# Cross-attention on one core: scaling the attended values instead of the exponentials

## The chip, the cores and the metric

The kernel runs on one core of a Trainium2 chip. The metric is device time in microseconds for one execution. The core has five engines that matter here: TensorE (PE in the profile, its weight loads PEld), VectorE (DVE), ScalarE (ACT), GpSimd (POOL) and SyncE (SP), which issues nearly all DMAs in the order of its own queue.

## The reference

A layer of cross-attention over 8 sequences of 256 rows, with 256 keys each, width 1024, 32 heads of 32, all in 32-bit floats:

```python
x = (hidden_states - mu) * rsqrt(var + LN_EPS) * ln_gamma + ln_beta
Q = split_heads(x @ Wq.T); K = split_heads(memory_keys); V = split_heads(memory_values)
scores = einsum('bhsd,bhtd->bhst', Q, K) * HEAD_DIM ** (-0.5)     # masked with -inf
probs = softmax(scores, axis=-1)
attn = einsum('bhst,bhtd->bhsd', probs, V)                        # heads joined again
out = hidden_states + attn @ Wout.T
```

Keys and values are the same tensor (the context).

## The kernel before, in words

**Quads.** Four heads of 32 fill the 128 partitions, so the unit of work is a quad of four heads of one sequence: 8 quads a sequence, 64 in all, numbered n = 8b + i. The main loop runs over n. Nothing is reordered by a scheduler: the order of each engine's queue is the order in which the program is written, and semaphores are set from the data that instructions share.

**One iteration n**, on TensorE: the scores of quad n + 1 (`scores`, L486, into four PSUM tiles `sc`), the attended values of quad n - 2 (`values`, L636, into two PSUM tiles `pv`), then parts of the query projection for a later sequence (L345 and L447) and of the output projection of the sequence before (`product_steps`, L720). From the second sequence on, both projections use a seven-product scheme on half-size blocks (names A11, S2, T4 and so on), whose sums of blocks POOL computes (`sum_x`, `sum_at`, `sum_wo`). The last sequence's output is made by `end_steps` (L787), partly in the last iterations (`po_last`) and partly after the loop (`po_end`, `po_end_s`).

**Softmax of quad n + 1** (`softmax_parts`), in the same iteration. For each head j and each half s of the rows, VectorE adds the mask and takes the row's extreme (L524), and ScalarE computes the exponentials `e` in place with their row sum `den` (`exps`, L528). `normalize(j)` takes the reciprocal of the sums (L535) and multiplies `e` by it, per partition: on POOL mostly (L543), on VectorE for j = 1 of quads 8 to 15, on ScalarE for j = 3 of quads 1 to 15 (L538). `blocks(j)` transposes the exponentials in blocks of 32 x 32 on VectorE into `pT` (L549). `aside` lets ScalarE copy half of `pT` to `pc` (L555), and `tail` issues the DMAs that exchange halves between partitions (`pT<-pT` L614, `pT<-pc` L618), with the loads of later keys, values and rows between them. In quads 0 to 7 and 57 to 63 the tail is put off into the next quad's softmax.

**Attended values.** `copy_at` lets ScalarE copy `pv` to `at` (L649), one iteration after the quad's softmax is complete. A tile `at` holds four quads (half a sequence), and it is the operand of the output projection.

**After the loop** TensorE works through products of the last sequence in written order: `values(61)`, `po_end` of quads 60 and 61, `values(62)`, `po_last`, `po_end_s` (from sums made by `end_sum` on POOL, L779), `values(63)`, and the rest. VectorE adds products to the rows (`end_add`, L793), and SP stores them (L1070).

## Time and profile before

| what | value |
|---|---|
| runs | 567.67, 567.94, 568.49 us (median 567.94) |
| profiled execution, first to last instruction | 566.0 us, granted clock of TensorE 1.000 |
| instructions | 20200 |
| chain that ended last | 97% TensorE |
| POOL multiplying exponentials by `rden` (L543) | 466 x 479 ns = 215.4 us |
| VectorE reciprocals (L535) | 256 x 150 ns = 38.2 us |
| ScalarE copies `at<-pv` (L649) | 128 x 253 ns = 26.1 us |

The profile page and the trace describe one execution, whose own time is the span in the table; the time of a run, measured around the execution, is 1.9 us more at the median. A row of groups reads: line, engine, operation, output <- input, shapes, count | busy us in all, mean ns of one | idle time before them and what ended it. A row of the timeline or of the chain begins with its start in us from the span's start and its duration; for a DMA on SP's queue (SPq) the duration is that of the issue, and the time to landing stands in the DMA views.

### The profile page before, as it was taken

What the parts mean: (1) busy time and instruction counts of PE and PEld (TensorE: products, weight loads), DVE (VectorE), ACT (ScalarE), POOL (GpSimd) and SP (SyncE); (2) the same over time, 40 slices, a digit from 0 to 9 for tenths busy, and PEclk for the clock granted to TensorE, in tenths of its full rate; (3) what the DMA queues carried; (4) which work ended last, traced back from release to release, by engine and by line L of the source; (5) the groups of instructions that cost most, each with busy time, mean ns of one, the idle gap of its engine ahead of it and who ended that gap; (6) DMA issues with size and microseconds to landing.
All of it is one profiled execution on the core that took longest, in us unless ns stands there. A gap on an engine that the chain in (4) does not pass through costs nothing.

```text
span 566.0 us, 20200 instructions
## 1 busy us (share of the span) xinstructions
PE 561.4 (99%) x7266; PEld 393.7 (70%) x7266; DVE 467.6 (83%) x1716; ACT 423.4 (75%) x1464; POOL 394.3 (70%) x636
## 2 busy tenths in 40 slices
PE   8999999999999999999999999999999999999997
PEld 8788886767766767667766776667766767755454
DVE  5889889999988988878898888988888777879923
ACT  4699999997778866786777876778776776769820
POOL 2788887899777656857568665777648657448780
PEclk9999999999999999999999999999999999999999
DMA  8966667856697777966778767796658864536751
GB/s 310 397 181 199 185 198 228 281 162 179 212 301 232 223 202 235 263 195 191 233 216 239 215 176 221 230 273 193 176 140 269 255 191 128 146 110 180 218 156 74
DMA packets 47219, 119.02 MB, mean 210 GB/s; under 512 B 8976, under 2 KB 9744, under 8 KB 47120
## 3 DMA queue, kind: packets, MB, share of 16 engines
q1 hardware_dynamic: 46976, 117.74, 69.5%
q8 instruction: 57, 0.93, 0.8%
q14 instruction: 42, 0.34, 0.2%
q10 hardware_dynamic: 144, 0.01, 0.0%
HBM read 66.33 MB, written 11.53 MB: 138 GB/s over the span
## 4 chain that ended last, share of the span: by engine, by line
PE 97%; DMA 1%; DVE 0%; POOL 0%; ACT 0%; issue 0%; SPq 0%; POOLq 0%
PE po_S L720 21%; PE pq_A L447 19%; PE pv L636 12%; PE sc L486 12%; PE po_A L720 11%; PE pq L345 9%; PE pq_S L447 8%; PE po_end L787 3%; PE po_last L787 1%; DMA x<-in_x_dram 1%; PE po_end_s L787 0%; POOL x L885 0%; PE pq L290 0%; PE px L307 0%; ACT e L528 0%; PE px L273 0%
## 5 line engine op out<-in xcount | busy, mean ns | idle before, releaser
L543 POOL TENSOR_SCALAR e<-e,rden 128x256 f32<-128x256 f32 x466 | 215.4, 479 | 125.5 <-DVE rden L535 123.0
L528 ACT ACTIVATE e<-e,mn 128x256 f32<-128x256 f32 x512 | 254.0, 502 | 46.1 <-DVE mn L524 44.9
L549 DVE STREAM_TRANSPOSE pT<-e 128x512 f32<-128x512 f32 x256 | 178.9, 703 | 35.6 <-POOL e L543 27.5
L524 DVE CUSTOM_DVE_ANT_0 e<-sc,mb 128x256 f32<-128x256 f32 x512 | 185.3, 415 | 25.4 <-PE sc L486 25.1
L555 ACT COPY pc<-pT 128x512 f32<-128x512 f32 x128 | 79.0, 617 | 55.7 <-DVE pT L549 35.6
L528 ACT ACTIVATION_READ_ACCUMULATOR e<-e,mn 128x1 f32 x512 | 98.4, 192 | 0.0
L486 PEld LDWEIGHTS sc<-k,qa 32*128 32x128 f32 x1024 | 46.1, 184 | 42.2 <-issue 21.6
L720 PE MATMUL po_S<-wo,at 128*128 128x512 f32 x152 | 74.3, 606 | 0.0
L636 PE MATMUL pv<-pT,v 64*32 64x128 f32 x4096 | 74.1, 274 | 0.0
L486 PE MATMUL sc<-k,qa 32*128 32x256 f32 x1024 | 73.6, 401 | 0.1
L636 PEld LDWEIGHTS pv<-pT,v 64*32 64x32 f32 x4096 | 57.0, 105 | 22.5 <-issue 11.8
L720 PE MATMUL po_A<-wo,at 128*128 128x512 f32 x128 | 59.4, 605 | 0.0
L345 PE MATMUL pq<-xnT,wq 128*128 128x256 f32 (+1 forms) x240 | 55.0, 384 | 0.0
L447 PEld LDWEIGHTS pq_A<-xnT,wq 128*128 128x128 f32 x416 | 48.5, 192 | 6.2 <-issue 4.8
L345 PEld LDWEIGHTS pq<-xnT,wq 128*128 128x128 f32 x240 | 44.6, 190 | 8.2 <-issue 1.5
L720 PE MATMUL po_S<-wo,s 128*128 128x512 f32 x104 | 50.1, 606 | 0.0
L447 PE MATMUL pq_A<-xnT,wq 128*128 128x128 f32 x416 | 48.5, 275 | 0.0
L535 DVE RECIPROCAL rden<-den 128x2 f32<-128x2 f32 x256 | 38.2, 150 | 7.3 <-ACT e L528 6.2
L524 DVE DVE_READ_ACCUMULATOR2_ANT mn<- 128x1 f32 x512 | 42.4, 83 | 0.0
L720 PEld LDWEIGHTS po_A<-wo,at 128*128 128x128 f32 x128 | 22.9, 189 | 25.6 <-issue 24.5
L720 PEld LDWEIGHTS po_S<-wo,at 128*128 128x128 f32 x152 | 25.5, 190 | 19.5 <-issue 19.5
L753 POOL TENSOR_TENSOR r<-r,p 128x512 f32<-128x512 f32 x24 | 30.6, 1277 | 4.8 <-ACT e L528 3.0
(102 smaller groups left out, 666.1 us busy)
## 6 DMA issues: line engine op xcount, KB each, us to landing
v<-in_kv_dram SPq DMA_DIRECT2D x32, 512.0 KB, 4.2
pT<-pT SPq DMA_DIRECT2D x128, 128.0 KB, 2.9
pT<-pc SPq DMA_DIRECT2D x128, 128.0 KB, 4.0
ring<-kept_T SPq DMA_DIRECT2D x20, 512.0 KB, 5.3
k<-in_kv_dram SPq DMA_DIRECT2D x32, 256.0 KB, 4.1
x<-in_x_dram SPq DMA_DIRECT2D x15, 512.0 KB, 5.6
r<-in_x_dram SPq DMA_DIRECT2D x28, 256.0 KB, 4.5
out_dram<-r SPq DMA_DIRECT2D x28, 256.0 KB, 3.2
```

What stands on the lines that cost most here:

```text
L345: nc.tensor.matmul(pqs[n], wq[:, o, c, :], xnTs[b](c), start=(c == 0), stop=(c == NC - 1),)
L447: nc.tensor.matmul(pqs[b][:, o, :], w[:, c], x_[:, c], start=begins and o + c == 0, stop=c == NK - 1, skip_group_check=True,)
L486: nc.tensor.matmul(scs[n][j][:, s, :], qa[r, n % NQ, ts(s, P)], ks[n - n % 2][r, n % 2, :], start=True, stop=True,)
L524: nc.vector.tensor_tensor_reduce(out=e[:, s, :], in0=pss[j][:, s, :], in1=mbs[n // NQ], scale=1.0, scalar=NO_SCORE, op0=ALU.add, op1=ALU.m ...
L528: nc.scalar.activation(e[:, s, :], e[:, s, :], AF.Exp, bias=mn[:, s : s + 1], scale=-1.0, accum_out=den[:, s : s + 1],)
L535: nc.vector.reciprocal(rden, dens[j])
L543: engine.tensor_scalar(es[j][:, s, :], es[j][:, s, :], rden[:, s : s + 1], 1.0, ALU.mult, ALU.mult,)
L549: nc.vector.transpose(pT[:, :, :, j, :, :].rearrange("p a i s k -> p (a i) s k"), es[j].rearrange("p s (b t) -> p b s t", t=K),)
L555: nc.scalar.copy(pc[:, :, ts(j, 2)], pT[:, 1, :, ts(j, 2)])
L636: nc.tensor.matmul(pvs[n][r][j * HD : (j + 1) * HD], vs[n - n % 2][ts(r, 2 * K), i, ds(n % 2 * P + j * HD, HD)], pT[ts(r, 2 * K), :, i, j, ...
L720: nc.tensor.matmul(po, operand(b, name)[:, c], wo[:, which, c], start=begins and c == 0, stop=c == NK - 1, skip_group_check=not begins,)
L753: nc.gpsimd.tensor_tensor(r, r, p1s[b], ALU.add)
```

## The change

Exponentials stay unscaled. The sums of four quads (128 rows x 4 heads x 4 quads x 2 halves) are collected in one tile `den`; when the fourth quad's sums are there, `send_dens` takes one reciprocal of 128 x 32, transposes it in blocks, writes it to a DRAM tile `sent`, and reads it back four times, once for each head, with each row given to the 32 partitions of that head, into `rB`. The attended values of a quad are multiplied by `rB` after they have been copied: in place on POOL (`scale_at`, quads 0 to 61), or on VectorE in place of ScalarE's copy (`copy_at_scaled`, quads 62 and 63). The products of `po_last` with quad 56 move from iteration 59 to iteration 60. `pc` has two buffers for three, and `rB` has one.

```diff
-    asp = ctx.enter_context(tc.tile_pool(name="asp", bufs=3))
+    asp = ctx.enter_context(tc.tile_pool(name="asp", bufs=2))
+    rbp = ctx.enter_context(tc.tile_pool(name="rbp", bufs=1))
...
+    dens, rBs = {}, {}
+    sent = dram.tile([P, K], F32, tag="sent", name="sent_dens")
...
+        h, quad = divmod(n, NK)
+        if quad == 0:
+            dens[h] = sm.tile([P, NH, NK, NS], F32, tag="den", name=f"den_{h}", bufs=2)
+        den = dens[h]
...
-                    accum_out=den[:, s : s + 1],
+                    accum_out=den[:, j, quad, s : s + 1],
...
-        def normalize(j):
-            rden = sm.tile([P, NS], F32, tag="rden", name=f"rden_{n}_{j}")
-            nc.vector.reciprocal(rden, dens[j])
...
+        def send_dens():
+            rden = sm.tile([P, K], F32, tag="rden", name=f"rden_{h}", bufs=1)
+            rdenT = sm.tile([P, K], F32, tag="rdenT", name=f"rdenT_{h}", bufs=1)
+            nc.vector.reciprocal(rden, den.rearrange("p j c s -> p (j c s)"))
+            nc.vector.transpose(rdenT, rden)
+            nc.sync.dma_start(sent, rdenT)
+            rBs[h] = rbp.tile([P, NA, NK, NS, K], F32, tag="rB", name=f"rB_{h}")
+            of = sent.rearrange("(a j i) k -> j a i k", a=NA, j=NH)
+            for j in range(NH):
+                nc.sync.dma_start(
+                    rBs[h][ts(j, HD)].rearrange("p a c s k -> p a (c s) k"),
+                    of[j : j + 1].to_broadcast([HD, NA, NK * NS, K]),
+                )
...
         blocks(2)
+        if quad == NK - 1:
+            send_dens()
...
+    def scale_at(n, engine):
+        h, c = divmod(n, NK)
+        at = ats[divmod(h, 2)][:, c]
+        engine.tensor_tensor(at, at, rBs[h][:, :, c].rearrange("p a s k -> p s a k"), ALU.mult)
+
+    def copy_at_scaled(n):
+        h, c = divmod(n, NK)
+        for r, pv in enumerate(pvs.pop(n)):
+            a = ts(r, 2)
+            nc.vector.tensor_tensor(
+                ats[divmod(h, 2)][:, c, :, a, :], pv.rearrange("p a s k -> p s a k"),
+                rBs[h][:, a, c].rearrange("p a s k -> p s a k"), ALU.mult,
             )
...
+        if n >= 2 and (n - 2) % NK:
+            for one in range(n - 3 if (n - 2) % NK == 1 else n - 2, n - 1):
+                scale_at(one, nc.gpsimd)
...
-            end_steps(last, "A11", B11, (c,), (0,))
+            for one in {0: (), 1: (0, 1)}.get(c, (c,)):
+                end_steps(last, "A11", B11, (one,), (0,))
...
     values(N - 2)
-    copy_at(N - 2)
+    copy_at_scaled(N - 2)
...
     values(N - 1)
-    copy_at(N - 1)
+    copy_at_scaled(N - 1)
```

All calls of `normalize` go with it. The order of the last four quads in time: quad 63's softmax lies in iteration 62, so `send_dens` of quads 60 to 63 is issued there; `scale_at(60)` and `scale_at(61)` stand in iteration 63, ahead of the remaining adds and sums on POOL; and TensorE's list after `values(61)` is as before.

More of the change, by code (lines that the diff above doesn't have):

```diff
@@ L495, in xattn_kernel @@
     tails = []
-    BY_ACT = range(1, 2 * NQ)
-    BY_DVE = range(NQ, 2 * NQ)
     def softmax_parts(n, copies=(), ahead=(), between=(), hooks={}, fill=()):
@@ L514, in softmax_parts @@
         pc = asp.tile([P, NI, NH, NS, K], F32, tag="pc", name=f"pc_{n}")
-        es, mns, dens = {}, {}, {}
+        es, mns = {}, {}
+        h, quad = divmod(n, NK)
+        if quad == 0:
+            dens[h] = sm.tile([P, NH, NK, NS], F32, tag="den", name=f"den_{h}", bufs=2)
+        den = dens[h]
         def exps(j, part=range(NS)):
@@ L520, in exps @@
                 mns[j] = sm.tile([P, NS], F32, tag="mn", name=f"mn_{n}_{j}")
-                dens[j] = sm.tile([P, NS], F32, tag="den", name=f"den_{n}_{j}")
-            e, mn, den = es[j], mns[j], dens[j]
+            e, mn = es[j], mns[j]
             for s in part:
@@ L529, in exps @@
                     e[:, s, :], e[:, s, :], AF.Exp, bias=mn[:, s : s + 1], scale=-1.0,
-                    accum_out=den[:, s : s + 1],
+                    accum_out=den[:, j, quad, s : s + 1],
                 )
-        def normalize(j):
-            rden = sm.tile([P, NS], F32, tag="rden", name=f"rden_{n}_{j}")
-            nc.vector.reciprocal(rden, dens[j])
-            for s in range(NS):
-                if j == NH - 1 and n in BY_ACT:
-                    nc.scalar.activation(
-                        es[j][:, s, :], es[j][:, s, :], AF.Copy, scale=rden[:, s : s + 1]
-                    )
-                    continue
-                engine = nc.vector if j == 1 and n in BY_DVE else nc.gpsimd
-                engine.tensor_scalar(
-                    es[j][:, s, :], es[j][:, s, :], rden[:, s : s + 1], 1.0,
-                    ALU.mult, ALU.mult,
+        def send_dens():
[10 more added lines that the diff above has]
+                    of[j : j + 1].to_broadcast([HD, NA, NK * NS, K]),
                 )
@@ L565, in softmax_parts @@
                 exps(j, (1,))
-            normalize(0)
             fill_in()
@@ L577, in softmax_parts @@
             exps(2)
-            normalize(0)
             exps(3)
@@ L591, in softmax_parts @@
             hook()
-        if n not in BY_DVE:
-            normalize(2)
         fill_in()
-        if n in BY_ACT:
-            normalize(3)
         blocks(1)
         aside(0)
-        if n not in BY_ACT:
-            normalize(3)
         fill_in()
         blocks(2)
+        if quad == NK - 1:
+            send_dens()
         while fill:
```

3 lines of the change are left out of this document (removed).

## The prediction

> **What bounds the kernel now.** I read the page first (span, busy shares, the chain), then the waits of TensorE, then the chain in order of time, and last the timeline of the end, engine by engine.
>
> ```profile
> span 566.0 us, 20200 instructions
> PE 561.4 (99%) x7266; PEld 393.7 (70%) x7266; DVE 467.6 (83%) x1716; ACT 423.4 (75%) x1464; POOL 394.3 (70%) x636
> PE 97%; DMA 1%; DVE 0%; POOL 0%; ACT 0%; issue 0%; SPq 0%; POOLq 0%
> ...
> PE busy L119 <- POOL ring masks.py:199: 1.3, 1, 1.3
> PE px L273 <- DVE ring L884: 0.2, 1, 0.2
> ...
> 286.89 1.91 PE po_S L720 x4
> 354.82 1.91 PE po_S L720 x4
> 422.75 1.92 PE po_S L720 x4
> ```
>
> TensorE is busy for 561.4 of 566.0 us, the chain that ends last is 97% TensorE, and its only two waits (1.3 and 0.2 us) lie in the first 7 us. A busy matmul can hide a stall, so I looked at the chain in order of time: the same product begins at 286.89, 354.82 and 422.75, twice 67.93 us apart. A stream that waited for other engines would not keep a period to the hundredth. I conclude that TensorE runs one fixed list of matmuls without a gap, and that the time is the length of that list plus some 3 us at the end. The change leaves that list as it is but for one step that comes one iteration later. So nothing that it takes from other engines can come back as time, and the question is only where it makes TensorE wait.
>
> **What is removed.** Times are those of the profiled execution.
>
> ```profile
> L543 POOL TENSOR_SCALAR e<-e,rden 128x256 f32<-128x256 f32 x466 | 215.4, 479 | 125.5 <-DVE rden L535 123.0
> L535 DVE RECIPROCAL rden<-den 128x2 f32<-128x2 f32 x256 | 38.2, 150 | 7.3 <-ACT e L528 6.2
> L538 ACT ACTIVATE e<-e,rden 128x256 f32<-128x256 f32 x30 | 13.6, 504 | 2.3 <-DVE rden L535 2.2
> ```
>
> All 512 scalings of exponentials go: 466 on POOL (215.4 us), 30 on ScalarE (13.6 us), 16 on VectorE; so do 256 small reciprocals (38.2 us). Each transpose of exponentials then waits for ScalarE alone. None of this is on the path: value in time, zero. TensorE covers it all.
>
> **What is added in the body.** For each of 16 groups of four quads: one reciprocal and one small transpose on VectorE, five DMAs on SP's queue (`sent`, then four broadcasts `rB` that wait until it has landed), and multiplications of attended values: 62 on POOL, and for the last two quads four on VectorE in place of ScalarE's copies.
>
> ```profile
> L779 POOL TENSOR_TENSOR ring<-at,at x1: 734/734/734, 543.7 to 543.7; 128x256 f32<-128x256 f32 x1
> ...
> 242.04 1.15 SPq L614 DMA_DIRECT2D pT<-pT  x2
> 246.47 2.00 SPq L618 DMA_DIRECT2D pT<-pc  x2
> 260.21 1.16 PE L636 MATMUL pv<-pT,v 64*32 64x128 f32 x64
> ...
> 514.70 1.14 SPq L614 DMA_DIRECT2D pT<-pT  x2
> 517.06 1.15 SPq L618 DMA_DIRECT2D pT<-pc  x2
> 525.49 1.16 PE L636 MATMUL pv<-pT,v 64*32 64x128 f32 x64
> 532.14 1.16 PE L636 MATMUL pv<-pT,v 64*32 64x128 f32 x64
> ...
> L549 DVE STREAM_TRANSPOSE pT<-e 128x512 f32<-128x512 f32 x256 | 178.9, 703 | 35.6 <-POOL e L543 27.5
> L555 ACT COPY pc<-pT 128x512 f32<-128x512 f32 x128 | 79.0, 617 | 55.7 <-DVE pT L549 35.6
> ```
>
> A POOL product of 128x256 takes 0.73 us, so 62 take 45 us against 215 removed: POOL becomes lighter. It stands still, though, once in each group, until `rB` has landed, with its sums queued behind. In the body those sums are due one to three iterations (67.93 / 8 = 8.5 us each) later and no longer stand behind six to eight scalings, so they come no later than now: zero.
>
> SP is the queue that is really moved past. While it waits for `sent`, the ring loads and the copies between partitions (`pT`, L614 and L618) of the same quad wait behind it. By the prices worked out below this holds SP some 2.0 + 4 x 0.57 = 4.3 us from the time the sums are ready; the copies would anyway have waited for the last transpose and ScalarE's copy of it (0.7 + 0.6 us), so they start 3 us late. Quad 27 stands for the twelve groups in mid-kernel: L618 ends its issue at 248.5, lands about 4 us later at 252.5 (the median of these copies, quoted below), and TensorE first needs it at 260.21. Three us late, and up to 2 us more behind the broadcasts' own 512 KB, gives 257.5: hidden with 2.7 us to spare. Quad 59 is tighter, because the iterations at the end take only 6.65 us (525.49 to 532.14): issue ends at 518.2, landing 522.3, needed at 525.49. SP is free of `sent` and `rB` at about 515.8 there, 1.1 us after L614's place now, so the landing moves to 523.4, or 525.4 with the extra traffic: hidden, by 0.1 to 2 us. The third copy buffer of `pc` that goes is then reused one quad earlier, 17 us after its last use began; only ScalarE would wait, off the path. If this cover were gone, each late quad would cost what it is late; that is a rival below.
>
> **What is added at the end.** Here the values of the last four quads cannot be scaled before quad 63's sums exist, and TensorE wants the first of them almost at once.
>
> ```profile
> 537.05 0.50 ACT L528 ACTIVATE e<-e,mn 128x256 f32<-128x256 f32 x1
> 537.45 0.19 ACT L528 ACTIVATION_READ_ACCUMULATOR e<-e,mn 128x1 f32 x1
> 537.72 1.16 PE L636 MATMUL pv<-pT,v 64*32 64x128 f32 x64
> 538.80 3.70 PE L787 MATMUL po_end<-wo,at 128*128 128x512 f32 x8
> ...
> 534.38 1.14 SPq L614 DMA_DIRECT2D pT<-pT  x2
> 536.63 1.95 SPq L618 DMA_DIRECT2D pT<-pc  x2
> ...
> out_dram<-x_again SPq DMA_DIRECT2D x1, 64.0 KB, 1.6
> ...
> pT<-pT SPq DMA_DIRECT2D x128, 128.0 KB, 2.9
> pT<-pc SPq DMA_DIRECT2D x128, 128.0 KB, 4.0
> v<-in_kv_dram SPq DMA_DIRECT2D x32, 512.0 KB, 4.2
> ...
> L1070 SPq DMA_DIRECT2D out_dram<-x_again x5: 332/332/332, 557.8 to 563.5; - x5
> ...
> DMA to landing us min/median/max: 2.2/2.3/4.9
> ```
>
> The last row is that of the `pT` copies between 505 and 545 us.
>
> At 538.80 TensorE begins the output products of quad 60 (`po_end`, L787). Now it must first see quad 60 multiplied by `rB`. The steps, each with its row:
>
> 1. Quad 63's last sum is read out at 537.45 + 0.19 = 537.64. These exponentials are paced by the scores before them, which TensorE delivers at the same time as now, so this stays.
> 2. Reciprocal and small transpose on VectorE: no row has a 128x32 transpose; between the small reciprocal's 0.15 and the 128x512 transpose's 0.7 us. Either way about 538.0 to 538.5, and SP is busy with quad 62's copies until 536.63 + 1.95 = 538.58. `sent` is issued at 538.6.
> 3. `sent`, 16 KB in rows of 128 B to DRAM. Nearest: the 64 KB output store, 1.6 us, alone on the DMAs; above it 2.9. Here the tail of L618 is still moving, so 2.0 us: 540.6.
> 4. Three more issues on SP at 1.14 / 2 = 0.57 us before the fourth broadcast goes: 542.3. The lower end is 0.33 us an issue, as SP's last output stores take.
> 5. Landing of 128 KB: 2.9 us is the median of the same size between partitions; 4.2, that of 512 KB, is what all four together could need, 2.2 the least seen at the end. I take 2.9: 545.2.
> 6. One POOL product, 0.73 us: 545.9.
>
> So TensorE stands from 538.80 to 545.9: 7.1 us. Ends: 538.6 + 1.6 + 1.0 + 2.2 + 0.73 = 544.1, a stall of 5.3; 538.6 + 2.9 + 1.7 + 4.2 + 0.73 = 548.1, a stall of 9.3. Below 5.3 the rows exclude it: two transfers in series and a product come after 537.64.
>
> [...]
>
> What follows is not late again.
>
> ```profile
> 540.05 2.50 POOL L746 TENSOR_TENSOR r<-r,ends 128x512 f32<-128x512 f32 x2
> 543.52 3.70 PE L787 MATMUL po_last<-wo,at 128*128 128x512 f32 x8
> 547.06 1.88 PE L787 MATMUL po_end_s<-wo,ring 128*128 128x512 f32 x4
> ```
>
> Quad 61's product is done 0.73 us after quad 60's, while quad 60's two products last half of the 3.7 us that the row of 538.80 shows for both quads. POOL's end sums now stand behind this wait: 545.9 + 0.7 (quad 61) + 2.5 (two residual adds) + 0.73 = 549.8, and TensorE asks for the first (`po_end_s`, now at 547.06) 8.3 us after `po_end` begins, so at 554.2. Quad 62 is multiplied on VectorE under the 3.7 us of `po_last`. So the whole tail moves by 7.1 us and nothing else grows.
>
> **The sum.** 0 in the body + 7.1 at the end. The profiled span becomes 573.1; the shown runs have their median 1.9 us above this span (567.94), which I keep: 575.0 us.
>
> **Rivals.**
>
> *A: the broadcasts clog the queue.* 128 partitions read the same 16 KB; if that takes some 3 us longer than step 5, the tail stalls by 10.1 and quad 59's copies are 1 to 3 us late for TensorE: about 567.94 + 10.1 + 2 = 580. From 3 us on, the mid-kernel quads stall too, by the excess over the 2.7 us spare, twelve times. For: no row shows a broadcast. Against: step 5's rows, where transfers of that size or four times it land in 2.2 to 4.9 us amid other traffic. Chance 0.11.
>
> *B: faster, because busy is not bound.* The row of TensorE's weight loads says 70%, and waits with other engines' names stand before them.
>
> ```profile
> PEld sc L486 <- DVE pT L549: 8.3, 11, 0.8
> PEld pv L636 <- ACT pc L555: 6.3, 19, 0.3
> PEld sc L486 <- DVE rden L535: 3.4, 5, 0.8
> PEld pv L636 <- ACT e L528: 2.7, 7, 0.8
> ```
>
> If these 20.7 us were true waits for the softmax, earlier transposes would return them, and 567.94 + 7.1 - 20.7 = 554.3. It decides from the point where more than 7.1 us of them is real. [...] This trace speaks against it: the unbroken period, and one quad's values taking 1.16 us at 260.21, 525.49 and 537.72, whatever went on beside them. The weight loads run beside matmuls and wait for their turn. Chance 0.04.
>
> *C: no change.* The broadcast is hidden, within 1.1 us. `rB` would have to land by 539.2, 1.5 us after the last sum; one transfer alone takes longer. Chance 0.03.
>
> **How the numbers follow.** Forecast 0.82, A 0.11, B 0.04, C 0.03. The forecast's own range is 567.94 + 5.3 to + 9.3, 573.2 to 577.2; I take it up to 578.5 for the mild half of A. Faster by over 0.2% (1.1 us, about what a measurement of this kernel can tell from no change) is B, 0.04; within it C, 0.03; slower 0.93.
>
> **What would show it.** In the changed profile: the period of 67.93 us unchanged; one TensorE wait of about 7 us before the first `po_end` product, released by POOL's multiplication of `at`; that one waiting for a DMA into `rB`; `sent` issued near 538.6; POOL busy some 170 us less. Wrong would be: TensorE idle before `pv` in the body (A), a shorter period (B), or no gap before `po_end` (C).

## The result, and the profile after

The changed kernel takes 610.8 us (median of 4 runs, 610.3 to 611.4) against 568.1 us for the kernel before (4 runs beside it, 567.7 to 568.5): a ratio of 1.075, 95% interval 1.0735 to 1.0766. The forecast was 575.0, range 573.2 to 578.5. The direction was right; the loss is 42.7 us, not 7.1.

The page of the changed kernel, its span, busy shares and the chain's shares:

```profile
span 608.5 us, 19634 instructions
PE 574.3 (94%) x7266; PEld 399.8 (66%) x7266; DVE 440.3 (72%) x1480; ACT 406.7 (67%) x1430; POOL 223.8 (37%) x232
PE 68%; DMA 16%; DVE 6%; ACT 3%; SPq 3%; issue 3%; POOL 2%; DVEq 0%; POOLq 0%; ACTq 0%
```

TensorE has the same 7266 matmuls, but the chain is 68% TensorE where it was 97%, and 16% of it is DMA. POOL is 170 us lighter, as forecast, and the kernel is slower. The chain in order of time shows at once that the loss isn't only at the end:

```profile
332.55 1.91 PE po_S L726 x4
405.07 1.91 PE po_S L726 x4
477.62 1.91 PE po_S L726 x4
```

The period of a sequence, 67.93 us before, is 72.5 us here. TensorE's waits, the two large rows of before being 1.3 and 0.2 us (columns: waiter, releaser, us in all, times, longest):

```profile
PE pv L628 <- DMA pT<-pc: 10.1, 7, 3.2
PE po_end L793 <- POOL at L648: 8.8, 1, 8.8
PE po_S L726 <- DVE r L768: 6.3, 7, 1.3
PE pq_S L448 <- DMA ring<-kept_T: 2.6, 2, 1.6
```

The wait of 8.8 us before `po_end` was forecast. The others were not: values that wait for the copies between partitions, output products that wait for the residual rows, query products that wait for ring loads. All three hang on DMAs of SP's queue that have nothing to do with the broadcast's data.

To split the loss I compare when TensorE begins the values of quad 61: at 537.72 before (the row is in the prediction), at 568.71 after.

```profile
568.71 1.16 PE L628 MATMUL pv<-pT,v 64*32 64x128 f32 x64
568.99 0.35 DVE L538 RECIPROCAL rden<-den 128x32 f32<-128x32 f32 x1 [0.27 <-ACT e L530]
569.37 0.21 DVE L539 STREAM_TRANSPOSE rdenT<-rden 128x32 f32<-128x32 f32 x1
569.61 0.33 SPq L540 DMA_DIRECT2D sent_dens<-rdenT  x1
573.08 1.76 SPq L544 DMA_DIRECT2D rB<-sent_dens  x4
577.86 1.41 POOL L648 TENSOR_TENSOR at<-at,rB 128x256 f32<-128x256 f32 x2 [12.33 <-DMA rB<-sent_dens]
578.63 6.37 PE L793 MATMUL po_end<-wo,at 128*128 128x512 f32 x8 [8.77 <-POOL at L648]
584.93 1.16 PE L628 MATMUL pv<-pT,v 64*32 64x128 f32 x64
```

568.71 - 537.72 = 31.0 us are lost in the body. The values of quad 62 began at 542.44 before and begin at 584.93 here, 42.5 us later, so the end costs 11.5 us more: the stand of 8.77, and 2.7 because the eight `po_end` products, 3.70 us before, take 6.37. After that nothing more is lost.

Below, "body" is always the start of the values of quad 61 less 537.72; "middle" is that part of it which arises between quads 9 and 57, where the groups of mid-kernel lie; and "end" is the further shift of the values of quad 62. Each is the difference of starts in two traces.

**Where the body loses it.** The timelines of the changed kernel on SP, TensorE and POOL behind the group that ends with quad 23:

```profile
223.08 0.33 SPq L540 DMA_DIRECT2D sent_dens<-rdenT  x1
225.22 1.74 SPq L544 DMA_DIRECT2D rB<-sent_dens  x4
...
232.35 3.76 SPq L333 DMA_DIRECT2D xnT<-xe  x6
...
241.80 2.33 SPq L606 DMA_DIRECT2D pT<-pT  x2
...
245.28 0.43 SPq L150 DMA_DIRECT2D r<-in_x_dram  x1
```

```profile
245.25 1.87 PE L628 MATMUL pv<-pT,v 64*32 64x128 f32 x64 [1.88 <-DMA pT<-pc]
...
253.67 0.70 PE L726 MATMUL po_S<-wo,s 128*128 128x512 f32 x1 [0.71 <-DVE r L768]
```

```profile
251.62 1.27 POOL L759 TENSOR_TENSOR r<-r,p 128x512 f32<-128x512 f32 x1 [6.25 <-DMA r<-in_x_dram]
```

The group itself holds SP 4 us (223.08 to 226.96), near the 4.3 forecast, and no product waits there. The bill comes two iterations later: six `xnT` copies, then the copies of the next quads, then the load of residual rows, all in SP's order. At 245.25 TensorE stands 1.88 us for a quad's copies; the residual load goes out at 245.28, POOL waits 6.25 us for it, VectorE for POOL, and TensorE for VectorE. In mid-kernel nearly all steps of the body lie at quads 8b + 7 to 8b + 9, around and after the group of quad 8b + 7. After the other group of a sequence TensorE loses nothing there.

SP's own stands, over the same four middle sequences, before (217.8 to 489.5 us) and after (226.2 to 519.9 us):

```profile
SPq L618 <- DMA pT<-pT: 37.7, 27, 4.5
SPq L614 <- ACT pc L555: 31.7, 19, 3.2
SPq L412 <- PE pq_A L447: 11.6, 7, 2.3
SPq L614 <- ACT e L528: 10.7, 8, 3.6
SPq L412 <- PE pq_S L447: 2.4, 2, 1.3
```

```profile
SPq L610 <- DMA pT<-pT: 62.5, 27, 6.0
SPq L544 <- DMA sent_dens<-rdenT: 14.0, 8, 2.7
SPq L606 <- ACT e L530: 9.4, 18, 1.1
SPq L606 <- ACT pc L556: 0.9, 2, 0.5
```

A stand for ScalarE (rows L614 before, L606 after) means that SP was early: it had nothing left to do but to wait for data. That slack was 31.7 + 10.7 = 42.4 us in four sequences, and 10.3 are left. The stands of ring loads for TensorE (rows L412) are slack of the same kind, since SP waits there for a buffer that is still in use: 11.6 + 2.4 = 14.0 us before, 1.1 after. Together 56.4 us of slack became 11.4. SP now stands 14.0 us for `sent` and 62.5 - 37.7 = 24.8 us more for landings of `pT`; its issues, added up over the four sequences, grew from 160 to 186 us. That is 65 us more in a queue that had 56 us to spare. 45 us of it were paid out of the slack; the other 20 are near the 293.7 - 271.7 = 22 us by which the four sequences became longer.

The windows of the same four sequences (columns: stretch, length, busy time of the five engines, granted clock, DMA share, GB/s), before, then after:

```profile
217.80:489.50 271.70, 271.70 (x3684) 192.17 (x3680) 226.69 (x837) 203.44 (x714) 182.35 (x316) 1.00 0.72 209
```

```profile
226.20:519.90 293.70, 278.85 (x3691) 195.54 (x3690) 211.66 (x722) 200.99 (x714) 88.60 (x94) 0.99 0.75 214
```

The 16 DMA engines were busy for 72% of the time before, a share that the prediction left out. 0.75 x 293.7 - 0.72 x 271.7 = some 25 us of their time were added.

### The profile page after: what moved, and what is told of

Read it like the earlier page. It is cut to its first block, busy times and chain, and to the rows that moved or that the text cites. A ratio compares the mean times of both kernels' runs of the same rounds, so it can differ in the third digit from the quotient of the medians.

```text
span 608.5 us, 19634 instructions
## 1 busy us (share of the span) xinstructions
PE 574.3 (94%) x7266; PEld 399.8 (66%) x7266; DVE 440.3 (72%) x1480; ACT 406.7 (67%) x1430; POOL 223.8 (37%) x232
## 4 chain that ended last, share of the span: by engine, by line
PE 68%; DMA 16%; DVE 6%; ACT 3%; SPq 3%; issue 3%; POOL 2%; DVEq 0%; POOLq 0%; ACTq 0%
PE po_S L726 18%; PE pq_A L448 16%; PE sc L489 8%; PE pv L628 8%; DMA r<-in_x_dram 6%; PE pq L346 5%; DMA ring<-kept_T 4%; PE pq_S L448 4%; PE po_end L793 3%; PE po_A L726 3%; ACT e L530 2%; DVE pT L550 2%; DMA pT<-pT 1%; DVE e L526 1%; SPq L606 1%
## 5 line engine op out<-in xcount | busy, mean ns | idle before, releaser
L526 DVE CUSTOM_DVE_ANT_0 e<-sc,mb 128x256 f32<-128x256 f32 x512 | 181.8, 418 | 56.2 <-PE sc L489 56.0
L550 DVE STREAM_TRANSPOSE pT<-e 128x512 f32<-128x512 f32 x256 | 167.8, 689 | 9.9 <-ACT e L530 9.8
L648 POOL TENSOR_TENSOR at<-at,rB 128x256 f32<-128x256 f32 x62 | 44.6, 731 | 241.8 <-DMA rB<-sent_dens 126.1
L628 PE MATMUL pv<-pT,v 64*32 64x128 f32 x4096 | 77.5, 274 | 11.1 <-DMA pT<-pc 10.1
L628 PEld LDWEIGHTS pv<-pT,v 64*32 64x32 f32 x4096 | 58.6, 105 | 35.8 <-issue 27.0
L726 PE MATMUL po_A<-wo,at 128*128 128x512 f32 x128 | 61.3, 621 | 0.0
L346 PE MATMUL pq<-xnT,wq 128*128 128x256 f32 (+1 forms) x240 | 54.9, 383 | 1.1 <-ACT qa L355 1.1
L526 DVE DVE_READ_ACCUMULATOR2_ANT mn<- 128x1 f32 x512 | 42.5, 83 | 0.0
L726 PEld LDWEIGHTS po_S<-wo,s 128*128 128x128 f32 x104 | 17.7, 189 | 21.7 <-issue 15.0
```

The source lines that it names most:

```text
L346: nc.tensor.matmul(pqs[n], wq[:, o, c, :], xnTs[b](c), start=(c == 0), stop=(c == NC - 1),)
L526: nc.vector.tensor_tensor_reduce(out=e[:, s, :], in0=pss[j][:, s, :], in1=mbs[n // NQ], scale=1.0, scalar=NO_SCORE, op0=ALU.add, op1=ALU.m ...
L550: nc.vector.transpose(pT[:, :, :, j, :, :].rearrange("p a i s k -> p (a i) s k"), es[j].rearrange("p s (b t) -> p b s t", t=K),)
L628: nc.tensor.matmul(pvs[n][r][j * HD : (j + 1) * HD], vs[n - n % 2][ts(r, 2 * K), i, ds(n % 2 * P + j * HD, HD)], pT[ts(r, 2 * K), :, i, j, ...
L648: engine.tensor_tensor(at, at, rBs[h][:, :, c].rearrange("p a s k -> p s a k"), ALU.mult)
L726: nc.tensor.matmul(po, operand(b, name)[:, c], wo[:, which, c], start=begins and c == 0, stop=c == NK - 1, skip_group_check=not begins,)
```

## The experiments

Two theories. **Q (queues):** the loss comes from instruction queues that stand for a landing with other quads' work behind them, SP above all, until the slack is spent. **Z (traffic):** it comes from the broadcasts' bytes, 512 KB twice a sequence, which stretch every other landing. Times are of single runs, each beside the kernel before on the same chip (568.2 to 570.5), unless a count is given. The expectations were written run by run, and their letters change: in c_nowait to e_split, S is SP's stand for the landing of `sent`, Q the broadcasts' bytes and P POOL's stand for `rB`; L is the time of SP's queue; in the runs whose names begin with f_, S is what is called Q here.

| kernel | time us | body | middle | end |
|---|---|---|---|---|
| the change | 610.8 (4 runs) | 31.0 | 27.1 | 11.5 |
| c_nodma | 569.25 | 1.1 | 0.1 | 0 |
| c_nowait | 592.71 | 17.0 | 16.4 | 7.9 |
| c_quarter | 603.31 | 24.6 | 20.8 | 10.9 |
| c_both | 578.75 | 4.4 | 3.6 | 6.5 |
| e_late | 617.63 | 38.3 | 22.5 | 11.4 |
| e_split | 606.0 | 26.8 | 20.8 | 11.4 |
| e_rearly | 610.86 | 31.8 | 29.4 | 11.3 |
| e_oldtail | 605.82 | 37.8 | 33.3 | 0 |
| t_dummy | 611.2 | 33.8 | 30.5 | 8.9 |
| e_actq | 611.03 | 31.8 | 27.5 | 11.4 |
| e_actq_oldtail | 605.5 (4 runs) | 37.5 | 32.7 | 0 |
| c_load | 784.06 | 202.9 | 168.0 | 0 |
| c_load6 | 619.27 | 48.9 | 43.1 | 0 |
| f_late_at | 601.26 | 22.4 | 9.3 | 10.9 |
| f_sp_next | 591.82 | 13.5 | 11.4 | 10.1 |
| f_actq_next | 591.46 | 12.7 | 9.3 | 10.6 |
| f_next_quarter | 580.68 | 2.6 | 0.7 | 9.9 |
| f_actq_next_oldtail | 581.01 | 13.0 | 6.2 | 0 |

One caution for reading it: e_rearly, e_oldtail and t_dummy leave the broadcasts in the twelve groups of mid-kernel as in the change, and their middle is 29.4, 33.3 and 30.5 against 27.1. Differences of less than some 6 us between single rows aren't read. Even that may be too fine for some kernels: the four runs of the change lie within 1.1 us, but those of e_actq_oldtail are up to 9.5 us apart.

**c_nodma: without the DMAs.**

```diff
-            nc.sync.dma_start(sent, rdenT)
-            rBs[h] = rbp.tile([P, NA, NK, NS, K], F32, tag="rB", name=f"rB_{h}")
-            of = sent.rearrange("(a j i) k -> j a i k", a=NA, j=NH)
-            for j in range(NH):
...
+            rBs[h] = rB_one
```

> The changed kernel without its DMAs: the reciprocals are made and transposed, but neither written to DRAM nor read back; POOL and VectorE multiply by a tile of ones, so nothing is normalised. It is the control for everything else in the change (POOL's products, the two buffers of pc, the moved step). Measured so far: TensorE is 31.0 us late at the values of quad 61, and the end adds 11.5 us. If all of that comes from the DMAs and what waits for them: span 566 to 568 us. If the third buffer of pc or POOL's products have a part, more than 570 us.

569.25 us (the kernel before took 570.45 beside it), and 1.1 us of body that arise at the start. Its windows over the four sequences:

```profile
217.80:489.50 271.70, 271.70 (x3681) 192.22 (x3680) 211.07 (x723) 201.36 (x714) 88.13 (x92) 1.00 0.74 212
```

The same 271.70 us, all of them TensorE, with POOL at half its work. (The DMA engines are at 74% without a single broadcast, so the share is known to some 2%.) So the removed scalings are worth nothing, and POOL's products, the two `pc` buffers and the step that moved cost nothing. The whole loss is five DMAs a group and the waits on them.

**c_nowait, c_quarter, c_both: the wait and the bytes.**

c_nowait reads input rows in place of `sent`:

```diff
-            of = sent.rearrange("(a j i) k -> j a i k", a=NA, j=NH)
+            of = x[0, 0:4, :].rearrange("q (r k) -> (q r) k", k=K)
+            of = of.rearrange("(a j i) k -> j a i k", a=NA, j=NH)
```

c_quarter, and c_both has both edits:

```diff
-                    rBs[h][ts(j, HD)].rearrange("p a c s k -> p a (c s) k"),
-                    of[j : j + 1].to_broadcast([HD, NA, NK * NS, K]),
+                    rBs[h][ts(j, HD), 0:1].rearrange("p a c s k -> p a (c s) k"),
+                    of[j : j + 1, 0:1].to_broadcast([HD, 1, NK * NS, K]),
```

> The same five DMAs in the same place of SP's queue, with the same bytes, but the four broadcasts read 16 KB of the input instead of the tile just written, so SP does not stand until that write has landed (the values are then scaled by other numbers). Theory S, SP standing for the landing (35.4 us in 16 waits) is what makes the copies and row loads behind it late: the body's 31 us fall to under 12, the end's stall falls by 2 to 3 us, span under 590. Theory Q, the broadcasts' bytes ahead of the copies on the DMA engines: body still 20 us or more, span over 595. Theory P, POOL standing for rB: rB comes some 2 to 3 us earlier, the body loses a little, span 598 to 605.

> All waits and issues of the change stay, but each broadcast moves a quarter of the bytes (only the first of four blocks of rB is filled, the rest stays at one). Theory Q: the body's 31 us fall to under 12, span under 590. Theory S: body still 20 us or more, span over 595. Theory P: like S.

> No wait for sent (broadcasts read the input) and a quarter of the bytes at once; the twenty issues a sequence stay. Alone the first left 17.0 us in the body and the second 24.6, from 31.0. If they add: 10 to 11 us, the end at 6 to 8, span 583 to 587. If both work on the same time of the queue: 14 to 17 us in the body.

Together with the change these are the four corners of a square. Body: wait and all bytes 31.0; wait and a quarter of the bytes 24.6; no wait and all bytes 17.0; no wait and a quarter 4.4. Taking the wait away is worth 14.0 with all bytes and 20.2 with a quarter; taking the bytes away 6.4 and 12.6. Each alone is worth less than it is with the other gone, as it would be where two loads share one slack. The 17.0 us of c_nowait lie between the bounds of its theories, and the 4.4 us of c_both below both forecasts. In these two kernels `rB` doesn't wait for `sent` either, so POOL gets it earlier: the 14.0 and 20.2 us hold SP's stand and POOL's, not SP's alone. The issue slots of the five DMAs, which stay in all four corners, cost no more than the 4.4 that is left.

**e_late, e_split: where the wait stands on SP.**

The four broadcasts become a function, `send_back`, called at the end of `tail`, behind the quad's own copies. In e_late this holds for all groups but the last, in e_split for those of mid-kernel that end with a quad 8b + 7 (`if behind`):

```diff
             for r in range(2):
                 nc.sync.dma_start(pT[ts(2 * r + 1, K), 0], pc[ts(2 * r, K)])
+            if quad == NK - 1 and n < N - 1:
+                send_back()
```

> The same result as the change, but the four broadcasts are issued after the quad's own copies between partitions (behind L610) instead of before them; sent keeps its place, so SP no longer stands for its landing with the copies behind it, and the copies are ahead of the broadcasts on the DMA engines too. The last group keeps its order. Theories S and Q: the body's 31 us fall to under 10, the end stays at 11.5, span 575 to 590. Theory P: rB lands some 8 us later, POOL's sums and adds come later, span 608 or more.

> The order of SP's queue mixed: in mid-kernel the broadcasts of a sequence's second four quads (last quad 8b + 7) go behind that quad's own copies, those of its first four (8b + 3) stay ahead as in the change; first, last groups as in the change. From the four runs so far: with all broadcasts ahead TensorE loses 4 to 6 us a sequence just after quad 8b + 7's sums (iterations 8b + 8 to 8b + 10) and nothing after 8b + 3's; with all behind it loses nothing there and 4.3 us after 8b + 3's, where POOL stands for rB with the shift of the row normalisation behind it. Theory S+P (two mechanisms, one for each place, each of them tied to one group): both go, the body's 31 us fall to 4 to 10, the end stays at 11 to 12, span 582 to 589. Theory of one shared cause (total bytes or SP's total load, with the order only moving the place where it shows): body still 20 us or more, span over 598.

e_late is slower than the change. Most of the loss at quads 8b + 7 goes, but a new one of about 4.4 us appears at quads 4, 20, 28 and 44 (8b + 4). ScalarE's and TensorE's waits in it:

```profile
ACT x L249 <- POOL shift L246: 41.3, 6, 8.7
```

```profile
PE pq_A L448 <- ACT xnT L458: 9.0, 4, 2.3
```

POOL asks for `rB` at the same place as before, now gets it later, and the row normalisation's `shift` stands behind that wait on POOL; ScalarE's normalisation and then TensorE's query products hang on it. e_split should have had the best of both and kept 26.8 us: moving the wait from one place in SP's queue to another in the same iteration isn't enough.

**e_rearly: the residual load ahead of the crowd.** The first load of residual rows of a sequence is issued one iteration earlier.

```diff
-            if i < 4:
+            if i in (1, 2, 3) or n == NQ:
                 between.append(partial(load_res, b, *((0, 0), (0, 1), (1, 1), (1, 0))[i]))
+            if i == NQ - 1 and b < B - 2:
+                between.append(partial(load_res, b + 1, 0, 0))
```

> The change with one load moved: the first residual block of each sequence (r 0,0) is issued one iteration earlier, ahead of the late stretch of SP's queue. In the change VectorE stood 35.0 us in six waits for POOL's add of that block, POOL in its turn 37.1 us in six waits for the load. If the late load alone closes the chain (store held in VectorE's queue, softmax late, copies late): body falls from 31 to under 15. If the copies pT are late by themselves: the waits of po_S for the store go (6.3 us), those of pv for pT stay (10 us) or grow, body 18 to 28, span 595 to 605.

The waits `po_S <- DVE r`, 6.3 us in the change, fell to 1.8 and those of `pv` for `pT<-pc` grew from 10.1 to 12.5; the time stayed, and the body is above both forecasts. The late residual load was an outlet of the loss, not its source.

**e_oldtail and t_dummy: the end.**

In e_oldtail quads 60 to 63 are normalised ahead of the transpose, as in the kernel before:

```diff
+        def normalize(j):
+            if h < N // NK - 1:
+                return
...
-        if quad == NK - 1:
+        if quad == NK - 1 and h < N // NK - 1:
             send_dens()
...
-    copy_at_scaled(N - 2)
+    copy_at(N - 2)
```

In t_dummy products whose result isn't used run ahead of the waiting one:

```diff
+    for _ in range(10):
+        end_steps(to_c22, "A11", B11, (0,), (0,))
```

> The change for 60 quads; quads 60 to 63 keep their exponentials normalised before the transpose (all on POOL), with plain copies of the attended values and no broadcast for them. If the 11.5 us at the end are the round trip of the last four quads: they go, body as in the change, span 595 to 599.

> The change with ten more products of full size (0.86 us each, result thrown away) for TensorE to run while it stands for quad 60's values at the end. The stand itself was 8.8 us, but the first eight po_end matmuls then took 6.37 us for 3.70, at a granted clock of 0.5. Theory G, a TensorE that stood idle for some us works at half clock afterwards: po_end is back at 3.7 us, the end costs 8.6 to 9.2 us and not 11.5, span 605 to 607 with the body as in the change. Theory that the first products are slow for another reason (their operands, the traffic of rB): po_end stays at 6.4, nothing gained.

In e_oldtail the end costs nothing, so all of the end's loss is the last group's broadcast. Its body came out at 37.8, against the expectation, which takes half of the gain back; e_actq_oldtail's is likewise 5.7 us longer than e_actq's. Both are near the spread named above, and I did not find a cause. In t_dummy the products fill the stand:

```profile
572.64 12.55 PE L793 MATMUL po_end<-wo,at 128*128 128x512 f32 x28
585.12 1.16 PE L628 MATMUL pv<-pT,v 64*32 64x128 f32 x64
```

28 products at 0.45 us (3.70 / 8 = 0.46 before), and the end falls from 11.5 to 8.9 (585.12 - 542.44 is 42.7, of which 33.8 is body). The end now costs what the 20 added products take (20 x 0.45 = 9.0 us), and the products of `po_end` behind them are not slowed. So the 2.7 us beyond the stand were the clock, which fell while TensorE stood: in the change the granted clock was 1.00 up to 573, 0.50 from 574 to 584 and 0.98 or more behind that; in t_dummy it was 1.00 from 560 to 585. The time didn't fall with it (611.2), because the body came out at 33.8.

**e_actq, e_actq_oldtail: another queue.** In mid-kernel the broadcasts are issued from ScalarE's queue, behind its copy `aside` of the same quad (in the second, with the end of e_oldtail).

```diff
             aside(1)
+            if behind:
+                send_back(nc.scalar)
```

> The change with the mid-kernel broadcasts (12 of 16 groups) issued from ScalarE's queue after its second copy of the quad; sent stays on SP, which no longer waits for its landing nor issues the four. Same bytes, same dependences, same sums. Theory L: SP is relieved of some 28 of the 65 us that were added in four sequences, the body's 31 us fall to 5 to 15, the end stays at 11.5, span 583 to 593. Theory of the bytes or of POOL's wait: body 25 us or more, span over 602. A body that stays although SP is relieved could also come from ScalarE standing for sent, which would show as waits of L548 on ScalarE's queue.

> Both cures together: mid-kernel broadcasts from ScalarE's queue, and the last four quads normalised before the transpose. Theory L: the end costs nothing and the body 5 to 15 us: 573 to 583 us. It cannot be faster than before, since TensorE's list of matmuls has the same length: if it is, the reading of the first profile was wrong.

SP is relieved (it stands 40.3 us for ScalarE's copy again, 41.9 before), yet the body is 31.8. The loss sits at other quads now, 8b + 6, and has another name. TensorE's largest wait, and the timeline of the engines around its second longest stand:

```profile
PE po_S L734 <- DVE r L776: 17.4, 7, 5.1
```

```profile
150.14 0.41 SPq L541 DMA_DIRECT2D sent_dens<-rdenT  x1
154.43 2.00 ACTq L548 DMA_DIRECT2D rB<-sent_dens  x4
156.53 0.51 ACT L531 ACTIVATE e<-e,mn 128x256 f32<-128x256 f32 x1 [8.97 <-issue]
157.65 0.71 DVE L554 STREAM_TRANSPOSE pT<-e 128x512 f32<-128x512 f32 x1 [4.10 <-ACT e L531]
158.29 0.65 DVE L776 TENSOR_TENSOR r<-po_S,r 128x512 f32<-128x512 f32 x1
158.99 3.78 PE L734 MATMUL po_S<-wo,at 128*128 128x512 f32 x4 [4.80 <-DVE r L776]
```

The expectation had named this rival: now ScalarE's queue stands for `sent`. Its broadcasts go out 4.3 us after SP issued `sent`, the next quad's exponentials are behind them, and ScalarE computes nothing for 8.97 us. (The profile calls that idle time `issue`, since the wait belongs to the DMA instructions ahead; for the broadcasts of 228.51 it names the landing of `sent`.) VectorE's transposes wait for the exponentials, the add of output products stands behind the transposes, and TensorE waits 4.80 us for that add. The same rows stand before 232.84, 304.80 and 379.09: ScalarE idle for 7.08, 6.22 and 9.29 us, TensorE for 2.89, 2.05 and 5.13. These four make 14.9 of the 17.4 us. The stand had moved from SP to ScalarE; it wasn't gone. A version with the old end measured 605.5 (600.0 to 609.5, ratio 1.060, interval 1.054 to 1.066). So Q in its simple form (SP alone) was refuted, and the traffic was still possible.

**c_load, c_load6: only hold SP.** c_nodma with 19, then 6, copies of 128 B from DRAM to DRAM on SP's queue at the place of the broadcasts.

```diff
+            for i in range(19):
+                nc.sync.dma_start(sent[i : i + 1, :], x[0, 0:1, ds(0, K)])
```

> The control without the change's DMAs (c_nodma, 567.1 us, nothing waits for rB, ones as factors) with SP's queue held in the same place: 19 tiny copies of 128 B between places in DRAM after each fourth quad, on which nothing depends. At about 0.4 us each they take some 8 us of SP per group, near what the change adds (over four sequences in mid-kernel: issues 160 to 186 us, landing of sent 0 to 14, landing of pT 38 to 62, so 65 us in 8 groups), with 0.04 MB and not 8.4 MB moved. Theory L, the time of SP's queue is what the body loses: TensorE late by 15 to 40 us at quad 61 again, no loss at the end, span 582 to 607. Theory of the bytes, or of POOL's wait for rB: under 5 us, span under 572.

> c_load with 6 tiny copies a group for 19: SP's queue is held some 4.4 us a group, about as long as by `sent`, its landing and four issues, with no bytes for SBUF and no rB; attended values are multiplied by ones, nothing is normalised. If holding SP's queue for that long is the cause: body 12 to 35 us, no stall at the end, 580 to 603 us. If the bytes of the broadcasts are: body under 5 us, below 574 us. (19 copies held it 15 us and lost 203 us.)

202.9 and 48.9 us, more than either theory allows. The timeline of SP in c_load6, and its windows over the stretch that the chain gives to these copies (262.92, 5.75 us):

```profile
261.66 3.11 SPq L544 DMA_DIRECT2D sent_dens<-in_x_dram  x5
264.87 1.00 SPq L415 DMA_DIRECT2D ring<-kept_B  x2
265.96 1.17 SPq L603 DMA_DIRECT2D pT<-pT  x2
```

```profile
262.90:268.70 5.80, 5.80 (x97) 4.64 (x80) 5.35 (x21) 5.80 (x21) 3.06 (x4) 1.00 0.65 11
```

In these 5.8 us the DMA engines moved 11 GB/s, although 1 MB of ring loads had been issued from 264.87 on and two copies of 128 KB from 265.96 on. So the transfers behind the tiny copies were held up, not only SP. These two kernels don't measure what they were meant to, and decide nothing between Q and Z. The trace of c_load6 has 12048 packets under 512 B and that of c_nodma 8976, 32 more for each of the 96 copies, so such a copy isn't one packet but 32. What held the ring loads back stays open.

**f_late_at, f_sp_next, f_actq_next: asking later.** The broadcasts are put where `sent` has landed, and POOL asks for `rB` one iteration later.
f_sp_next issues those of mid-kernel one iteration later, first in the next quad's `tail`; f_actq_next in the same iteration behind `aside(1)`, from ScalarE's queue; f_late_at at e_late's place. f_sp_next:

```diff
         def tail():
+            while backs and not behind:
+                backs.pop()()
             blocks(3)
```

On POOL, all three:

```diff
-        if n >= 2 and (n - 2) % NK:
-            for one in range(n - 3 if (n - 2) % NK == 1 else n - 2, n - 1):
+        put_off = range(NQ + 2, N - NQ + 1)
+        if n >= 2 and (n - 2) % NK and not ((n - 2) % NK == 1 and n in put_off):
+            first = n - 3 if (n - 2) % NK == 1 else n - 2
+            if (n - 2) % NK == 2 and n - 1 in put_off:
+                first = n - 4
+            for one in range(first, n - 1):
                 scale_at(one, nc.gpsimd)
```

> e_late (broadcasts behind the quad's own copies) with POOL's multiplication of the first two quads of a group one iteration later. e_late lost 38 us in the body, seen at quads 8b+4, where the row normalisation's shift stood behind POOL's wait for `rB`. Theory S: that place goes, body 5 to 20 us, 583 to 599 us, period near 69 to 71 us. Rival Z: 30 us or more remain, over 608 us.

> As f_actq_next, but the broadcasts are issued from SP's queue, one iteration after the sums, ahead of the next quad's copies between partitions, where SP would stand for the last transpose anyway. Theory S: SP has four issues of 0.43 us more a group (3.5 us a sequence, against a slack of some 10 us) and stands for nothing: body 2 to 12 us, 581 to 592 us. If SP's issue time alone were enough: body as in the change, 27 to 38 us, over 605 us. Rival Z: over 596 us, and the same as f_actq_next.

> In the twelve groups of mid-kernel the broadcasts are issued one iteration later, from ScalarE's queue behind its copy of the next quad (by then `sent` has landed, so that no queue stands for it), and POOL multiplies the first two quads of a group one iteration later, together with the third. The first two groups and the last two stay as in the change. Theory S (queues that stand for a landing with other work behind them): no queue stands any more, only the broadcasts' bytes are left, body at most 10 us later than before, end still 11.4 us: 580 to 589 us. Rival Z (the traffic itself, 512 KB twice a sequence, stretches the landings of whatever is beside it): the body still loses 17 us or more, over 596 us.

The middle falls from 27.1 to 9.3, 11.4 and 9.3 us: the same number whichever queue issues and wherever. All the bytes are still moved. f_late_at's total is above its expectation because it puts the groups at the start and near the end behind too, where it loses 8.6 and 4.5 us. f_actq_next's 591.46 is 2.5 above its bound; f_sp_next's time is inside and its body 1.5 above. So some two thirds of the middle's loss is queues that stand, as Q says. It isn't SP alone: e_late had made POOL's stand longer, and e_actq had moved SP's to ScalarE. In f_sp_next SP has no stand for `sent` left in mid-kernel, while POOL stands for `rB` as long as ever (127.8 us in the whole kernel, 126.1 in the change). No run moves POOL's multiplication alone, so how the two thirds are divided between SP and POOL isn't shown.

**f_next_quarter: what is left.** f_actq_next with a quarter of the bytes, edited as in c_quarter.

> f_actq_next with a quarter of the bytes in each broadcast (as in c_quarter: the multiplier is correct for one block of rows only, elsewhere the values are multiplied by ones or by other quads' reciprocals). f_actq_next kept 12.7 us in the body. If that is the broadcasts' bytes (in before, DMA engines are already 72% busy over the four middle sequences; f_actq_next: 79%): body 1 to 5 us here, 578 to 584 us with the end's 11 us. If it is the number of DMAs, or POOL's later multiplication: 9 us or more, over 586 us.

Body 2.6, middle 0.7. What was left were the bytes, Z's part. The windows of the middle in f_actq_next and in f_next_quarter:

```profile
222.00:499.00 277.00, 273.77 (x3680) 193.12 (x3679) 213.66 (x727) 200.49 (x714) 87.21 (x92) 0.99 0.79 224
```

```profile
222.00:489.00 267.00, 266.72 (x3592) 189.24 (x3591) 208.85 (x710) 198.17 (x703) 87.13 (x91) 1.00 0.74 216
```

With all bytes the DMA engines are 79% busy and TensorE is idle for 3.2 of these 277 us; at 74%, c_nodma's share, for 0.3 of 267 us (a slightly shorter piece of the same work).

**f_actq_next_oldtail: body and end together.**

> f_actq_next with the last four quads' exponentials normalised ahead of the transpose as before (as in e_oldtail), so that nothing stands at the end. If body and end are independent: 12.7 us in the body and 0 at the end, 579 to 584 us. In e_oldtail and e_actq_oldtail the body grew by 6 us when the end was taken away: if that comes back, 585 to 590 us. Slower than the kernel before either way, since the bytes are still there.

581.01 us: 13.0 in the body, 0 at the end, and the body did not grow this time. It is the fastest version that normalises every value, 30 us better than the change and still 12.8 us slower than the kernel before (568.17 beside it). No version of the idea that I tried beats that, because what it saves was never on the path.

## Why the prediction was wrong, step by step

**What bounds the kernel: right, and half of it.** TensorE is the bound before; c_nodma confirms that removing 170 us from POOL and 38 us of reciprocals is worth nothing, as said under "What is removed". (A busy matmul did hide time in the change: the 64 products at 393.34 were busy for 1.53 us at a granted clock of 1.00, 1.16 before. And a stream that waits can keep its period: the change's three rows above are 72.52 and 72.55 us apart.) But TensorE with one unbroken list says only that every other resource keeps up. How narrowly was not asked. SP had 56 us of slack in four sequences, and the DMA engines were at 72%.

**"Zero in the body": the step that failed, by 31 us.** It was put as: SP is held 4.3 us once a group, the copies of quad 27 come 3 us late, and 2.7 us are to spare. Three things in it fell.
- SP was held 4 us, and the copies of that quad were in time: the local sum was right. But the delay doesn't end with that quad. It stays in the queue until the queue is idle, and it was checked against one deadline, in the group that ends with 8b + 3. In the group that ends with 8b + 7 the `xnT` copies, the ring loads and the residual loads of the next sequence follow. The sum to make was a whole sequence's: added issues and stands against the stands that are slack.
- "Up to 2 us more behind the broadcasts' own 512 KB" priced the bytes once. They also come back as time that SP stands for landings: over four sequences the `pT<-pT` row is 62.3 us with all bytes and no wait for `sent` (c_nowait), 41.0 with a quarter of them (c_both). The wait does it too, 54.9 with a quarter of the bytes (c_quarter), so the growth from 37.7 to 62.5 isn't the bytes' alone. By f_actq_next and f_next_quarter the bytes cost some 9 us of the middle when no broadcast stands for `sent`.
- "It stands still once in each group, with its sums queued behind ... so they come no later than now: zero" leaves out who waits for POOL. e_late shows `shift` behind that stand and TensorE behind `shift`; with POOL's multiplication moved as well (f_late_at against e_late) the middle fell from 22.5 to 9.3. What this stand costs in the change itself isn't measured.

**`pc` with two buffers: zero, right** (c_nodma).

**The end: right in its steps, with one term missing.** The last sum's reciprocal is ready and `sent` goes out 0.9 us after the values of quad 61 begin, 568.71 to 569.61, as forecast (537.72 to 538.6). That is partly luck: the forecast had it wait for SP's copies, and here SP is free at 569.21 and the transpose ends last, at 569.58. `sent` to the broadcasts' issue: 573.08 - 569.61 = 3.5 us, 2.0 forecast. Their issue 0.44 us each, 0.57 forecast. From the end of the last issue to POOL's product 577.86 - 574.84 = 3.0, 2.9 forecast. The product 0.7. The stand is 8.77 us, 7.1 forecast, inside 5.3 to 9.3, and most of the miss is `sent`. The missing term is the clock, 2.7 us: it was granted at 0.57 from 578.60 to 585.00, and at 1.00 in the kernel before from 537.70 to 542.50. The broadcasts behind this `sent` went out 3.5 us after it; the median landing of the 16 was 1.8:

```profile
sent_dens<-rdenT SPq DMA_DIRECT2D x16, 16.0 KB, 1.8
rB<-sent_dens SPq DMA_DIRECT2D x64, 128.0 KB, 3.1
```

All 16 have the same size and the same rows of 128 B, so something else made this one late, and what it was isn't shown.

**Rival A named the mechanism at 0.11 and gave it the wrong trigger and price.** "The broadcasts clog the queue", TensorE idle before `pv`, was what happened. But it was to decide from the point where a broadcast lands 3 us later than 2.9; it lands in 3.1. The queue clogged at the very landing time that was forecast. And at 580 it was still priced by one deadline twelve times, not by a queue's budget.

**Rival B** (busy is not bound) is refuted by c_nodma: half of POOL's work gone, VectorE 16 us lighter in the four sequences, and the same 271.70 us of TensorE, with the weight loads busy beside its products for 192.2 us in both.

**What stays open.** The split between stands and bytes is known to some 6 us, the spread of the middle among kernels with the same DMAs there. Whether the body really grows in e_oldtail and e_actq_oldtail, by 6.8 and 5.7 us, and not in f_actq_next_oldtail, is not known. Nor is by which way the bytes make TensorE late when no broadcast stands for `sent`: f_next_quarter shows that they do, not how.

## What to carry to other kernels

A bound engine without a gap says nothing about how close the next resources are (here TensorE was 99% busy, and SP had 56.4 us of slack in four sequences, of which the change left 11.4): for each queue that a change loads, add issues and stands over a whole period, and compare with the time that the queue now stands because it is early. A delay in an in-order queue is due at every deadline behind it until the queue is idle (SP was held for 4 us from 223.08 on, and TensorE stood for a copy at 245.25), so the place to check is the most crowded stretch of the period, not the one after the edit. When a wait has to be added, put its instruction where the data has already landed, on every queue that asks for it; moving only one of the askers moved the loss (the body is 31.0 us in the change and 31.8 in e_actq).

## What the runs showed of the hardware

**The clock fell after some stands.** Windows of the changed kernel around the stand of 1.88 us that ends at 245.25 (the granted clock is the third number from the end):

```profile
245.20:247.00 1.80, 1.75 (x64) 1.26 (x64) 1.03 (x6) 1.46 (x4) 0.17 (x1) 0.76 0.95 279
247.00:248.80 1.80, 1.80 (x8) 0.84 (x3) 0.00 (x0) 1.80 (x10) 0.00 (x0) 0.50 0.99 363
248.80:250.20 1.40, 1.40 (x10) 1.28 (x9) 0.00 (x0) 1.40 (x7) 0.00 (x0) 0.74 1.07 247
```

Counted from these shares, TensorE ran at half clock for 0.9 + 1.8 + 0.7 = 3.4 us in all here. It happened once more in the body, behind a stand of 3.17 us that ends at 320.03 (0.80 from 320 to 322, 0.50 from 322 to 324). Behind the stand of 2.16 us that ends at 393.34 the granted clock stayed at 1.00, so the length of the stand alone didn't decide it. At the end TensorE stood for 8.77 us: the clock was 1.00 up to 573 and 0.50 from 574 to 584, and the products of 3.70 us took 6.37: 2.7 us were lost beyond the stand.

**Ring loads crawled behind tiny copies.** Behind six copies of 128 B, with ring loads issued from 264.87 on, the DMA engines moved 11 GB/s until 268.7 (c_load6).

**Another queue bought no bandwidth.** f_actq_next and f_sp_next differ in the queue that issues the broadcasts, ScalarE's or SP's, and in its place within the quad's `tail`: 591.46 and 591.82 us, and from 222 us on, over 277 and 278 us, the DMA engines were 79% and 78% busy and moved 224 GB/s in both.
